# Image 0's query and key convolutions by a two-level scheme

## The chip, the cores and the metric

One core of a Trainium2 chip runs the whole program in one launch. The metric is device time in microseconds: lower is better. Times of before are the median of three runs; a profiled execution shows what each engine did.

## The reference, cut to what matters

Eight images of 512 channels and 32 x 32 = 1024 places go through two attention blocks, all in fp32. The first block has 32 groups in its norm and 8 heads, the second 8 groups and one head.

```python
# block 0
h = group_norm(x, gn_weight, gn_bias)                      # 32 groups
qkv = einsum('oc,bct->bot', w_qkv, h) + b_qkv              # 3 x 512 by 512, a matrix product per image
q, k, v = per head (64 channels each)
weight = softmax(einsum('bct,bcs->bts', q * scale, k * scale))
a = einsum('bts,bcs->bct', weight, v)
x = x + einsum('oc,bct->bot', w_proj, a) + b_proj
# block 1, one head of 512 channels
xn = group_norm(x, gamma, beta)                            # 8 groups
q, k, v = conv1x1(xn, q_w), conv1x1(xn, k_w), conv1x1(xn, v_w)
x = x + conv1x1(softmax(q @ k * scale) @ v, p_w)
```

What the change touches is the product of the 512 x 512 query and key weights with the normed image 0 (512 x 1024) in block 0.

## The kernel before

**Matrix products in halves.** Every large product uses Winograd's form of Strassen's scheme: both operands are cut into 2 x 2 quarters, sums of quarters are made (four sums for each operand), and seven products of quarters take the place of eight; the results are added up on the way out of PSUM. The sums are named by the product they serve: for weights 1 is a11, 2 is a12, 3 is s4, 4 is a22, 5 is s1, 6 is s2, 7 is s3 (`left_sums`); for images 1 is b11, 2 is b21, 3 is b22, 4 is t4, 5 is t1, 6 is t2, 7 is t3 (`right_sums`). `ORDER = (1, 5, 2, 6, 7, 3, 4)` is the order in which they lie in a weight tile.

*Once in halves:* `conv` (through `by_channel` and `wino`) does a convolution in seven steps, each of four matmul calls of 512 columns, that is eight matmul records in the trace. `by_token` does the same for the values, with tokens on the rows. `wino` takes a list of steps (`middle`), runs some entries of the `background` list after each step (`back` of them), and leaves its steps 4 and 3 on a list `tail`, which the next stage runs after its own first step (`finish()`).

*Twice in halves:* `conv2` splits each of the seven products again in seven: 49 products of a 128 x 128 weight with 256 columns. It takes them in four groups (`pair`): products 1 and 5 together, then 2 and 6, then 7 with 3 and 4 begun inside it, each group with seven inner steps (`inner_steps`). `hooks[s]` are functions that run after group s (s = 0, 1, 2 and 3; in the code the group of 3 and 4 is s = 3 and that of 7 is s = 2). Its image factors come from `inner_factors` (L434): four subtractions of 128 x 256 for each of the seven outer factors. Its weight factors are second sums, which lie in DRAM (`wdram2`) and are loaded in two parts by `load_weight`. Some results are added together by GpSimd (`more`, L571), the others by VectorE (L564, L566) from PSUM, and ScalarE adds the bias halves (L578).

**Before, image 0 is the exception.** The prologue holds it: the image's values, queries and keys are computed once in halves, since their second sums are made only there. `prepare(n)` loads a weight into one of three slots of `wpool` and gives four steps on VectorE for the first sums (L291, L292). `keep2` makes the second sums (four `tensor_tensor` of 128 x 896, L318, into tiles of their own) and stores seven parts of 448 KB in DRAM for the later images: v's on VectorE, q's, k's, m's and p's on GpSimd. All later images use `conv2`.

**The prologue in order.** Raw k and q weights, image 0 and the v, q and k weights are loaded; k and q are transposed (`natural`), the norm's statistics are taken, and the product m of q and k weights is made (`product`). Then the value convolution, the query convolution, the key convolution; meanwhile image 1's statistics (`x1`, L91) and the sums of m. Then the value weights are transposed (`tr_wv`), the bias products are made from natk, raw p and raw p0 (`bias_products`), then the product z, and the attention of image 0 starts.

**What sets the order.** A scheduler places the instructions of each engine ahead of the run; the order on each engine is fixed then. Whatever is wrapped in `keep_in_program_order` stays behind what was traced before it on its engine. All matmuls are wrapped, so PE runs in the written order. Loads and stores go through SP's queue. Working tiles of 4 KB a partition come from a pool `big` of `NBIG = 34`.

```python
tail.extend([lambda: step(4), lambda: step(3), *after])          # wino: left to the next stage
w = weights2[s // 2][:, (0, 2, 0, 1)[s] :]                       # conv2: weights from the loaded tiles
```

## Time and profile before

| | |
|---|---|
| median of 3 runs | 2768.14 us (2767.19 to 2768.42) |
| profiled execution, its own time | 2768.3 us |
| its span | 2765.8 us |
| PE busy | 2753.6 us |
| VectorE (DVE) busy | 2045.6 us |
| GpSimd (POOL) busy | 1291.4 us |
| ScalarE (ACT) busy | 998.4 us |
| value convolution of image 0 | 25.25 to 49.50 us |
| query and key convolutions of image 0 | 49.50 to 97.56 us |
| first attention of image 0 starts | 117.85 us |

In the profile PE is the matmul unit, PEld its weight loads, SP the engine that issues most DMAs. A row of the order of time has start, length, engine, line, operation, `out<-in`, the shape, and in brackets the idle time before it with what ended it. A row of waits has the total, the number and the longest. A row of stretches has the stretch, its length, then busy time (and instructions) of PE, PEld, DVE, ACT and POOL, the granted clock, DMA's busy share and GB/s. All matmuls have line L60 and all transposes L63, so they are told apart by the tiles they write: `psa_q`, `psb_q` and `psc_q` are the PSUM banks of the query convolution, and so on.

### The profile page before, as it was taken

The numbers are of one execution on the slowest core, as the hardware profiler recorded it, in microseconds if no ns is written. First come the engines' busy times: TensorE is split into PE (matmuls) and PEld (weight loads), VectorE is DVE, ScalarE is ACT, GpSimd is POOL, SyncE is SP. The second block draws the span as 40 slices with busy tenths as digits, with TensorE's granted clock in tenths as the row PEclk, the third lists the DMA queues.
The fourth block names the chain that finished last, engine by engine and source line by source line (L and its number), as shares of the span: only waits on it lengthen the run. The fifth ranks groups of instructions, "written<-read, shape, count | busy, mean of one in ns | idle before, by whom it ended". The sixth has DMA issues, their size and how long they took to land.

```text
span 2765.8 us, 36809 instructions
## 1 busy us (share of the span) xinstructions
PE 2753.6 (100%) x13436; PEld 1762.1 (64%) x13436; DVE 2045.6 (74%) x3214; ACT 998.4 (36%) x1307; POOL 1291.4 (47%) x1384
## 2 busy tenths in 40 slices
PE   9999999999999999999999999999999999999999
PEld 5437736776376853868538694486844968348585
DVE  6587777777777777777777867777678776787776
ACT  1253454214632146312453125531255313633130
POOL 2313605745067440774307752176621766146763
PEclk9999999999999999999999999999999999999999
DMA  7827412344113441144401443114521145112302
GB/s 265 253 91 252 181 32 70 138 159 166 40 63 138 170 162 32 63 161 167 150 24 63 177 182 119 32 55 184 196 98 49 58 153 216 59 54 97 142 24 74
DMA packets 126070, 332.60 MB, mean 120 GB/s; under 512 B 19831, under 2 KB 64695, under 8 KB 114362
## 3 DMA queue, kind: packets, MB, share of 16 engines
q1 hardware_dynamic: 125294, 329.75, 33.6%
q8 instruction: 108, 1.77, 0.3%
q14 instruction: 80, 0.66, 0.1%
q10 hardware_dynamic: 588, 0.42, 0.1%
HBM read 258.14 MB, written 71.99 MB: 119 GB/s over the span
## 4 chain that ended last, share of the span: by engine, by line
PE 99%; DVE 1%; DMA 0%; issue 0%; SPq 0%; DVEq 0%
PE sc L60 16%; PE av L60 16%; PE psb_av L60 6%; PE psb L60 5%; PE psa_av L60 4%; PE psc_av L60 4%; PE psc L60 4%; PE psa L60 3%; PE psb_v L60 3%; PE psb_k L60 3%; PE psb_p L60 3%; PE psb_q L60 3%; PE psb_g L60 3%; PE psb_z L60 3%; PE psc_z L60 2%; PE psa_k L60 2%
## 5 line engine op out<-in xcount | busy, mean ns | idle before, releaser
L700 DVE TENSOR_TENSOR sum<-sum,e 128x1024 f32<-128x1024 f32 x384 | 473.9, 1234 | 35.5 <-ACT e L696 0.9
L696 ACT ACTIVATE e<-sc 128x1024 f32<-128x1024 f32 x512 | 476.1, 1053 | 63.1 <-PE sc L60 62.6
L60 PE MATMUL sc<-q,k 64*128 64x512 f32 x2048 | 456.8, 596 | 0.0
L60 PE MATMUL av<-e,v 128*64 128x512 f32 x2048 | 453.4, 595 | 0.0
L60 PEld LDWEIGHTS sc<-q,k 64*128 64x128 f32 x2048 | 190.1, 185 | 245.9 <-ACT e L696 120.9
L60 PEld LDWEIGHTS av<-e,v 128*64 128x64 f32 x2048 | 141.4, 137 | 299.0 <-issue 288.2
L434 POOL TENSOR_TENSOR inner_h<-x 128x256 f32<-128x256 f32 x16 | 14.8, 924 | 415.9 <-DVE x L1028 415.9
L698 DVE TENSOR_TENSOR sum<-e,e 128x1024 f32<-128x1024 f32 x64 | 79.9, 1249 | 103.6 <-ACT e L696 103.6
L719 ACT COPY a<-av 128x512 f32<-128x512 f32 x64 | 37.5, 586 | 320.1 <-PE av L60 280.6
L126 POOL TENSOR_TENSOR rstd<-ve,mhalf 128x4 f32<-128x4 f32 x16 | 18.8, 1177 | 274.0 <-DVE ve L124 274.0
L60 PE MATMUL psb<-inner,inner_h 128*128 128x256 f32 x448 | 115.6, 380 | 0.0
L60 PE MATMUL psa_av<-e,z 128*128 128x512 f32 x256 | 112.5, 592 | 0.0
L482 ACT COPY psb_v<-psa_v 128x512 f32<-128x512 f32 (+1 forms) x28 | 14.5, 517 | 232.5 <-DVE x L845 176.6
L60 PEld LDWEIGHTS psb<-inner,inner_h 128*128 128x128 f32 x448 | 84.5, 190 | 13.6 <-POOL inner L449 2.1
L60 PE MATMUL psb_z<-w_z,inner_h 128*128 128x128 f32 x672 | 87.5, 276 | 0.0
L60 PE MATMUL psb_g<-inner_h,w_m 128*128 128x256 f32 x336 | 84.9, 381 | 0.0
L776 ACT ACTIVATE e<-e 128x1024 f32<-128x1024 f32 x64 | 65.1, 1052 | 46.7 <-DVE e L766 25.6
L60 PEld LDWEIGHTS psb_z<-w_z,inner_h 128*128 128x128 f32 x672 | 81.4, 192 | 0.5
L60 PEld LDWEIGHTS psa_av<-e,z 128*128 128x128 f32 x256 | 47.4, 190 | 53.6 <-issue 51.7
L771 POOL TENSOR_TENSOR e<-e,e 128x512 f32<-128x512 f32 x64 | 79.3, 1271 | 2.0 <-DVE e L766 1.8
L571 POOL TENSOR_TENSOR v<-v,v 128x256 f32<-128x256 f32 x28 | 20.1, 726 | 125.3 <-DVE u_v L566 121.3
L820 POOL TENSOR_TENSOR t<-e,t 128x1024 f32<-128x1024 f32 x32 | 78.4, 2482 | 0.0
(443 smaller groups left out, 6138.0 us busy)
## 6 DMA issues: line engine op xcount, KB each, us to landing
r<-all_rows SPq DMA_DIRECT2D x78, 256.0 KB
x<-in_x SPq DMA_DIRECT2D x36, 512.0 KB
h<-in_x SPq DMA_DIRECT2D x32, 512.0 KB
spill<-x SPq DMA_DIRECT2D x32, 512.0 KB
x<-spill SPq DMA_DIRECT2D x32, 512.0 KB
out<-x SPq DMA_DIRECT2D x63, 256.0 KB
kept<-a SPq DMA_DIRECT2D x28, 512.0 KB
again<-kept SPq DMA_DIRECT2D x28, 512.0 KB
```

The source lines that it names most:

```text
L60: tc.keep_in_program_order(nc.tensor.matmul(*args, **kw))
L126: nc.gpsimd.tensor_tensor(rstd, ve, mhalf, ALU.pow)
L434: pin(engine.tensor_tensor(dst, x, y, ALU.subtract))
L482: nc.scalar.copy(ps["b"], ps["a"])
L571: nc.gpsimd.tensor_tensor(d, x, y, ALU.add)
L696: nc.scalar.activation(e, sc, AF.Exp, scale=(C // 8) ** -0.5)
L698: nc.vector.tensor_add(total, es[0], e)
L700: nc.vector.tensor_add(total, total, e)
L719: nc.scalar.copy(dst, av)
L771: nc.gpsimd.tensor_tensor(blocks(dst, r, cc)[0], blocks(x, r, cc)[0], blocks(y, r, cc)[0], ALU.add)
L776: nc.scalar.activation(e[c, cc, r], e[c, cc, r], AF.Exp, scale=scale)
L820: on = lambda *a: lambda: tc.keep_in_program_order(nc.gpsimd.tensor_tensor(*a))
```

## The change

- q and k of image 0 are computed by `conv2`, with the weights' second sums taken from SBUF, where they have just been made (`own`), and not from DRAM. No weight is loaded for it.
- The image's inner factors (7 x 4 subtractions of 128 x 256) are made by GpSimd while PE does the value convolution.
- `keep2_steps` becomes `second_sums`: with `inside=True` it puts the sum s3 in the place of a21 and takes three tiles of `big` for the others, and it also returns a function that picks a factor. q's second sums move from GpSimd to VectorE, into the value convolution; k's stay on GpSimd, in the hooks of the query convolution; v's move from VectorE to GpSimd, in the hooks of the key convolution.
- k's first sums move from the query convolution into the value convolution (`back` is 6, not 4).
- Image 1's loads move into the query convolution's second hook, its statistics into the third, in halves; the raw v and p loads and m's loads move into the key convolution's second hook, m's first sums into its fourth.
- `NBIG` is 35, not 34, and the identity takes the place of a line of sums (`rpool`). `all_background` is defined earlier.

```diff
-NBIG = 34
+NBIG = 35
...
-        def keep2_steps(n, t, engine=nc.gpsimd, pin=lambda ins: ins):
-
-            if engine is nc.gpsimd:
-                u = wpool.tile([P, 4, 7, P], F32, tag="w", name=f"prepare2_{n}")
-                u = [u[:, i, :, :] for i in range(4)]
-            else:
-                u = [big_tile(f"prepare2_{n}_{i}", (P, 7, P)) for i in range(4)]
+        def second_sums(n, t, engine, pin=lambda ins: ins, inside=True):
+
             quarter = lambda k, i: t[:, :, k, ts(i, P)]
             a11, a21, a12, a22 = quarter(0, 0), quarter(0, 1), quarter(1, 0), quarter(1, 1)
-            s1, s2, s3, s4 = u
+            if inside:
+                s3 = a21
+                s1, s2, s4 = (big_tile(f"prepare2_{n}_{i}", (P, 7, P)) for i in range(3))
+            else:
+                u = wpool.tile([P, 4, 7, P], F32, tag="w", name=f"prepare2_{n}")
+                s1, s2, s3, s4 = (u[:, i, :, :] for i in range(4))
+            f2 = (a11, a12, s4, a22, s1, s2, s3)
+
             def store():
-                for j, f in enumerate((a11, a12, s4, a22, s1, s2, s3)):
+                for j, f in enumerate(f2):
                     pin(nc.sync.dma_start(wdram2[n][:, :, j, :], f))
 
-            return [
+            return lambda p, j: f2[j - 1][:, ORDER.index(p), :], [
...
-        def conv2(n, f, bias, name, hooks=(), after=(), by_tokens=False, alone=False):
+        def conv2(n, f, bias, name, hooks=(), after=(), by_tokens=False, alone=False, own=None):
...
-                w = weights2[s // 2][:, (0, 2, 0, 1)[s] :]
+                def weight_of(i, j):
+                    if own:
+                        return own(products[i], j)
+                    return weights2[s // 2][:, (0, 2, 0, 1)[s] + i, j - 1, :]
...
-            ident.append(big_tile("ident", (P, P)))
+            ident.append(rpool.tile([P, 2, 2, P], F32, tag="line", bufs=1, name="ident")[:, 0, 0, :])
...
-            raw_v = raw("v", 6)
-            raw_p = raw("p", 7)
             for f in first["v"][1]:
                 f()
-            background.extend(steps)
-            background.extend(first["q"][1])
-            v = by_token(weight_factors(first["v"][0]), hf, "v0_0", middle=(2, 5, 6, 7), back=4)
+            in_order = tc.keep_in_program_order
+            inner, ih = inner_factors(hf, "h0_0", in_order)
+            wq2, q_sums = second_sums("q", first["q"][0], nc.vector)
+            background.extend([*steps, *first["q"][1], *ih[:2], *q_sums[:4], *first["k"][1], *ih[2:], q_sums[4]])
+            v = by_token(weight_factors(first["v"][0]), hf, "v0_0", middle=(2, 5, 6, 7), back=6)
+            all_background()
+            norm1, x1, made = GroupNorm(0, "0_1"), [], {}
+
+            def load_x1():
+                x1.extend(load_x(1, c, "x1") for c in range(KC))
+
+            def half_stats(c, i):
+                norm1.half_stats(c, i, x1[c][:, ts(i, HT)])
+                if i:
+                    norm1.end_stats(c)
+
+            def stats():
+                background.extend(lambda c=c, i=i: half_stats(c, i) for c in range(KC) for i in range(2))
+
+            def load_raw():
+                made["v"], made["p"] = raw("v", 6), raw("p", 7)
+
+            def prepare_m():
+                made["m"] = prepare("m")
+
+            def sum_m():
+                for f in made["m"][1]:
+                    f()
+
+            wk2, k_sums = second_sums("k", first["k"][0], nc.gpsimd)
+            q = conv2("q", inner, pcols("bq0"), "q0_0", [k_sums[:2], [load_x1], [*k_sums[2:], stats]], own=wq2)
+            _, v_sums = second_sums("v", first["v"][0], nc.gpsimd)
+            k = conv2(
+                "k", inner, pcols("bk0"), "k0_0",
+                [v_sums[:2], [all_background, load_raw, prepare_m], v_sums[2:], [sum_m]], own=wk2,
+            )
             finish()
-            run_background(len(background))
-            keep2("v", first["v"][0], nc.vector)
-            background.extend(first["k"][1])
-            x1 = [load_x(1, c, "x1") for c in range(KC)] if B > 1 else []
-            norm1 = GroupNorm(0, "0_1")
-            background.extend(lambda c=c: norm1.stats(c, x1[c]) for c in range(len(x1)))
-            q = conv(weight_factors(first["q"][0]), hf, pcols("bq0"), "q0_0")
-            keep2("q", first["q"][0])
-            keep2("k", first["k"][0])
-            t, steps = prepare("m")
-            k = conv(weight_factors(first["k"][0]), hf, pcols("bk0"), "k0_0", hooks=[[], [], [], [], steps])
-            finish()
+            raw_v, raw_p, t = made["v"], made["p"], made["m"][0]
```

More of the change, by code (lines that the diff above doesn't have):

```diff
@@ L219, in run_background, with all_background @@
                 background.pop(0)()
+        def all_background():
+            run_background(len(background))
         tail = []
@@ L325, in keep2_steps, with keep2 @@
             ]
-        def keep2(n, t, engine=nc.gpsimd):
-            for f in keep2_steps(n, t, engine):
+        def keep2(n, t):
+            for f in second_sums(n, t, nc.gpsimd, inside=False)[1]:
                 f()
@@ L585, in written @@
                     return [(t, 2 * i + r) for t, (i, _) in zip(to, y)]
-                w = weights2[s // 2][:, (0, 2, 0, 1)[s] :]
+                def weight_of(i, j):
+                    if own:
+                        return own(products[i], j)
+                    return weights2[s // 2][:, (0, 2, 0, 1)[s] + i, j - 1, :]
                 def mm(ps, j, start):
                     for i, p in enumerate(products):
-                        wt = w[:, i, j - 1, :]
+                        wt = weight_of(i, j)
                         if not by_tokens:
@@ L613, in conv2 @@
             second = []
-            weights2 = [weight_part((n, 0))]
+            load = [] if own else [load_weight]
+            weights2 = [] if own else [weight_part((n, 0))]
             pair(0, (1, 5), [(1, 0), (1, 1)], None, [])[1]()
             pair(
-                1, (2, 6), [(0, 0), (0, 1)], [(1, 0), (1, 0)], [load_weight, lambda: biased_half(0, 0)], defer=second,
+                1, (2, 6), [(0, 0), (0, 1)], [(1, 0), (1, 0)], [*load, lambda: biased_half(0, 0)], defer=second,
             )[1]()
-            weights2.append(weight_part((n, 1)))
+            if not own:
+                weights2.append(weight_part((n, 1)))
             ahead, end = pair(
-                3, (3, 4), [(0, 1), (1, 0)], [(0, 1), (1, 0)], [load_weight, *after],
+                3, (3, 4), [(0, 1), (1, 0)], [(0, 1), (1, 0)], [*load, *after],
                 order=(-3, 6, 5, -4, 7, 2) if alone else (-3, 6, -4, 2, 5, 7),
@@ L991, in prologue @@
             load = lambda: load_weight(tc.keep_in_program_order)
-            second = keep2_steps("z", t, pin=tc.keep_in_program_order)
+            _, second = second_sums("z", t, nc.gpsimd, tc.keep_in_program_order, False)
             later = {
@@ L1011, in load_again @@
             return t
-        def all_background():
-            run_background(len(background))
         def begun(load, norm, b, what):
```

## The prediction

> **What bounds the kernel.** I read the engine shares first, then PE's waits over the whole span, then PE's order of time around image 0's convolutions, then the table of stretches. Shares of the page, PE's waits, three rows of PE's order of time (start, length), and stretches (length, then busy time of each engine):

> ```profile
> PE 2753.6 (100%) x13436; PEld 1762.1 (64%) x13436; DVE 2045.6 (74%) x3214; ACT 998.4 (36%) x1307; POOL 1291.4 (47%) x1384
> ...
> PE tr_wk L63 <- DMA rawk<-in_w: 3.8, 1, 3.8
> PE tr_wv L63 <- DVE k L410: 0.5, 1, 0.5
> PE ps_wm L60 <- DVE natq L900: 0.5, 1, 0.5
> PE psb_v L60 <- DVE u_v L566: 0.5, 1, 0.5
> ...
> 49.50 3.60 PE L60 MATMUL psa_q<-h,prepare_q 128*128 128x512 f32 x8
> 52.93 3.60 PE L60 MATMUL psb_q<-t_h,prepare_q 128*128 128x512 f32 x8
> ...
> 97.56 0.49 PE L63 MATMUL tr_wv<-ident,rawv 128*128 128x128 f32 x3
> ...
> 49.50:97.56 48.06, 48.06 (x113) 21.23 (x112) 32.55 (x44) 5.09 (x8) 18.01 (x8) 1.00 0.81 258
> ...
> 277.74:298.89 21.15, 21.15 (x99) 18.62 (x98) 16.49 (x36) 6.52 (x11) 20.03 (x28) 1.00 0.42 152
> ```

> PE is busy almost throughout, and its longest wait after the first load is 0.5 us; all other engines run beside it. So only removed PE work saves time, and at most some 2 us of waits could go besides. Image 0's query and key convolutions fill 49.50 to 97.56: 14 steps, one every 3.43 us. The last line is image 1's query convolution, which already has the form of the change (halves twice): 21.15 us from its first product to that of the next one, with no PE wait in it.

> [...]so I price PE by the distance from one convolution's start to the next, not by busy time. [...]the trace shows 0.69 and 1.08 to 1.09 us, so I use the trace's. [...]DVE, then GpSimd, in order of time:

> ```profile
> 55.04 0.69 DVE L240 TENSOR_TENSOR u_q<-psb_q,t_q 128x512 f32<-128x512 f32 x1
> ...
> 58.13 4.46 DVE L292 TENSOR_TENSOR prepare_k<-prepare_k 128x512 f32<-128x512 f32 x2
> ...
> 232.91 2.35 DVE L1028 TENSOR_TENSOR t_h<-h,t_h 128x512 f32<-128x512 f32 x2
> 235.19 1.75 DVE L734 TENSOR_TENSOR a<-a,r 128x1024 f32<-128x1024 f32 x1
> ...
> 54.66 9.87 POOL L318 TENSOR_TENSOR prepare_q<-prepare_q 128x896 f32<-128x896 f32 x4 [29.40 <-DMA sums_v<-prepare_v]
> ...
> 233.66 1.06 POOL L434 TENSOR_TENSOR inner_h<-h,inner_h 128x256 f32<-128x256 f32 x1
> 234.68 1.17 POOL L434 TENSOR_TENSOR inner_h<-h,h 128x256 f32<-128x256 f32 x1
> 235.82 1.70 POOL L434 TENSOR_TENSOR inner_h<-h,inner_h 128x256 f32<-128x256 f32 x1
> ```

> Two SBUF sums of DVE that take 1.29 us alone take 4.46 beside GpSimd; a GpSimd inner subtraction takes 0.72 alone (as at 237.49), 1.17 when it alternates with a 512-column DVE sum and 1.70 with a 1024-column one. The sum at 55.04 reads PSUM and keeps its 0.69[...].

> **The change, part by part.**

> *PE.* Removed: 2 x 7 steps x 3.43 = 48.06 us. Added: 2 x 49 products of 256 columns; one such convolution takes 21.15 us, so 42.30. Net -5.76 us, if nothing is late. All the rest can only take from this. The first products of the new query convolution run before the last two steps of the value convolution, near 42.6; those two take 6.9 us, so the key convolution ends near 42.6 + 6.9 + 42.3 = 91.8, and the transposes of the value weights start there instead of at 97.56.

> *GpSimd, in 25 to 55.* Added: 7 x 4 inner subtractions. GpSimd is idle there (its first work after 25.3 is at 54.66). Alone they take 28 x 0.72 = 20.2 us. The first two groups are needed at 50.5 (the value steps hide them), the next two at about 55, the last three from 60: even with all 14 DVE sums of the stretch between them they end near 55, so PE does not wait for them.

> *DVE, in 25 to 50.* Added: q's four second sums, 4 x 1.0; k's four first sums move here, 4 x 0.6. Removed: v's four second sums at 50.3 to 54.5 go to GpSimd. DVE has room (13.4 us busy of the 25 from 25 to 50)[...]: from 25.7, 10 sums of 512 columns at 1.17 and four of 896 at about 1.6 (between 1.17 and 1.70) end at 43.8 instead of 35.7. The eviction of step 6 comes ready at 37.68 and PE reuses that bank at 39.14, a slack of 0.77 us after its 0.69. If evictions, which are not pinned to the order, are put between the sums, they come at most about one locked sum late: 0 to 1 us. If all sums stand ahead of them: 43.8 - 37.7 - 0.77 = 5.3 us. No gain is possible here, as PE has no wait to lose. I take 0.4, range 0 to 5.3.

> *DVE in the query convolution.* Such evictions take 12.4 us of 21 (image 1's key convolution); x1's statistics add 8 x 0.62 + 4 x 0.2 = 5.8. Image 1's value convolution carries such statistics too and lost 0.17 + 0.45 us to late evictions. I take 0.3, range 0 to 0.8; ACT and the bias adds hide behind PE as in image 1.

> *GpSimd, 55 to 92.* k's and v's second sums, four of 2.08 us each, and 2 x 8 additions of 0.73: 16.6 + 11.7 = 28 us of the 37 up to 92, so there is room; k's third and fourth sums, behind q's additions, should be ready near 70 and are needed near 74 and 76. Cost nothing; a lag of over 4 us would show.

> *SP and its transfers.* No byte is added. In before the raw value and projection weights are issued from 22.66 and 26.38, and nothing moves from 42 to 51. These (2 MB, 5.8 us at the 360 GB/s that weight loads reach) now go behind x1's loads, k's stores and x1's statistics, whose tiles they take over: x1 issued near 58, landed near 66, counted by 78; raw value weights issued near 81 and landed by 86, the projection's near 89, m's by 92. Needed: 91.8 and 94.4. Covered by 3 to 6 us. The third load, raw p0, is issued from 90.44 in before; it stands behind the layer-0 projection's tile, which needs one of three weight slots: q's goes to m, v's comes free only when its sums are stored, k's when the key convolution ends. If it is issued ahead of that, it lands by 94; if behind it, at 96 to 98, and the bias products, all pinned in PE's order and the next PE work after the transposes, wait from 94.4. I take 0.5, range 0 to 6. Stores of q's sums move earlier (near 44 to 50, where nothing moved before).

> *After 118.* The first attention starts about 5 us earlier; image 1's loads do not all move. ACT's scaling of h waits 0.68 us for them at 141.23, and ACT's next copy is at 146.13: 3.7 us of slack hide most of it. 0, range -0.5 to 1. The larger tile pool, the moved identity and the shared closure: 0, nothing on PE waits for a big tile in before; the gap of 0.5 at the transposes stays, as the same banks are emptied.

> Sum: -5.76 + 0.4 + 0.3 + 0.5 = -4.6 us, against the profiled execution's 2768.3 (its span 2765.8 and 2.5 around it). That execution stands 0.16 over the median of 2768.14, so 2763.5.

> **Rivals.** [...]DVE's pinned sums stand ahead of the value convolution's evictions, +5.3 instead of +0.4, which gives 2768.4. For it: 14 sums against 28 subtractions in one stretch; against: evictions are free to move up, and in before they were put between k's first sums (55.04, 57.53).

> *Transfers come last and it is slower.* Place: bias products, on raw p0, behind a weight slot. GpSimd is some 6 us late, ends v's sums at 96, their four stores (448 KB at the 290 GB/s of such stores, 1.6 us each) free the slot at 102, two loads of 2.9 us land raw p0 at 108 to 110, PE waits about 15: -5.8 + 15 gives 2777. It decides from a landing at 94.4 + 5.8 = 100.2 (no gain) and 105.7 (slower by 0.2%). For it: in before raw weights were in place long ahead; against: 28 us of DMA idle before 145 and stores of unchanged quarters that can go early.

> *It does not cut PE:* if the pairs of 256-column products ran slower with weights out of strided tiles, nothing would change, 2768. Image 1's 21.15 us speaks against it.

> **How the numbers follow.** A measurement of this kernel can tell about 0.2%, 5.5 us, so even the full -5.76 barely counts as faster. As summed, with up to 1.2 us more or less: 0.55, of which 0.33 lies beyond -5.5 (all waits near zero). Still better through small waits gone, to -6.6: 0.03. Part or all lost to lock or a late load, 2765 to 2771: 0.27. Slower by transfers: 0.12. No cut: 0.03. So faster 0.36, same 0.52, slower 0.12. The range goes from 2761.5 (-6.6) to 2769.5, which leaves out the slower rival and the end of the third case.

> **What would show it.** Right: q and k products of 128x256 in 42.3 us, transposes of the value weights near 92, inner subtractions of 0.72 to 1.7 us ending near 55, no PE wait over 1 us. Wrong: a PE wait at psb_v for u_v (lock), at tr_wv or ps_bias for a raw weight (transfers), at psa_k to psc_k for k's sums (GpSimd).

## The result, and the profile after

The changed kernel takes 2782.99 us (median of 6 runs, 2780.71 to 2784.70) against 2768.28 us: ratio 1.0053, 95% interval 1.0040 to 1.0066. It is slower by 0.5%, and the prediction of 2763.5 us was wrong in sign and size. The profiled execution's own time is 2784.7 us, its span 2782.9.

First the engine shares of the page, then PE's waits over the whole span (total, number, longest):

```profile
PE 2756.7 (99%) x13520; PEld 1785.5 (64%) x13520; DVE 2061.2 (74%) x3254; ACT 1007.7 (36%) x1323; POOL 1333.5 (48%) x1428
```

```profile
PE tr_wv L63 <- DVE k L569: 5.2, 1, 5.2
PE tr_wk L63 <- DMA rawk<-in_w: 4.7, 2, 3.9
PE psb_v L60 <- DVE u_v L243: 4.6, 1, 4.6
PE psb_k L60 <- ACT psb_k L487: 2.2, 1, 2.2
PE psc_v L60 <- DVE x L855: 1.7, 2, 1.0
```

There is less product work, yet PE is *busier* than before (2756.7 against 2753.6 us). Three waits are new: 4.6 us in the value convolution, 2.2 near the start of the key convolution, 5.2 at the transposes. They make 12 us. The rest is in how long the matmuls behind them take. PE's order of time:

```profile
45.50 5.96 PE L60 MATMUL psb_v<-prepare_v,h 128*128 128x256 f32 x16 [4.59 <-DVE u_v L243]
...
55.62 3.62 PE L60 MATMUL psc_v<-prepare_v,h 128*128 128x256 f32 x16
...
83.52 1.37 PE L60 MATMUL psb_k<-inner_h,prepare_k 128*128 128x256 f32 x4 [2.19 <-ACT psb_k L487]
...
111.44 3.44 PE L63 MATMUL tr_wv<-ident,rawv 128*128 128x128 f32 x15 [5.23 <-DVE k L569]
```

The 16 matmuls behind the first wait take 5.96 us; 16 of the same shape take 3.62 ten us later. The stretches say why; the granted clock is the third number from the end (then DMA share and GB/s):

```profile
58.20:105.94 47.74, 45.14 (x197) 37.89 (x196) 30.51 (x71) 12.39 (x21) 23.56 (x21) 0.96 0.56 178
...
39.84:43.25 3.41, 1.07 (x5) 0.59 (x4) 3.38 (x4) 0.00 (x0) 3.33 (x3) 1.00 0.90 275
43.25:46.67 3.42, 1.17 (x3) 0.99 (x4) 3.41 (x5) 0.00 (x0) 3.42 (x4) 0.50 0.96 287
46.67:50.08 3.41, 3.41 (x10) 2.70 (x9) 3.39 (x4) 0.00 (x0) 3.33 (x4) 0.50 0.94 283
50.08:53.49 3.41, 3.41 (x18) 3.00 (x17) 2.46 (x4) 0.00 (x0) 3.33 (x6) 1.00 0.92 283
...
80.80:84.21 3.41, 1.22 (x6) 0.80 (x5) 2.84 (x8) 1.80 (x3) 3.30 (x3) 1.00 0.82 224
84.21:87.63 3.42, 3.42 (x9) 2.70 (x9) 0.00 (x0) 1.17 (x2) 2.07 (x1) 0.50 1.05 347
...
104.69:108.11 3.42, 1.52 (x7) 0.84 (x6) 3.42 (x5) 0.72 (x1) 3.42 (x3) 1.00 0.65 194
108.11:111.52 3.41, 0.08 (x1) 0.11 (x2) 3.19 (x5) 0.72 (x1) 2.65 (x3) 0.50 1.01 291
111.52:114.93 3.41, 3.41 (x17) 3.41 (x17) 0.66 (x2) 0.44 (x1) 3.33 (x3) 0.50 1.00 330
```

The stretches of 3.41 us are cut where the granted clock changes. Each of the three waits is followed by half clock, for 6.83, 3.41 and 6.83 us. Part of that time lies in the waits themselves; after PE has started again, at 45.50, 83.52 and 111.44, 4.58, 3.42 and 3.49 us of it are left. From start to start two matmuls of 128x256 take 0.86 us there (`psa_k`, 84.68 to 85.54) and 0.44 at full clock (88.73 to 89.17), so half of that is lost: some 2.3, 1.7 and 1.7 us (an estimate from these times).

The first line stands for the query and key convolutions: 47.74 us where the prediction had 42.30. It begins 0.87 us ahead of `psb_q` at 59.07, as four records of the query convolution have already run among the value convolution's last steps.

Laying the two traces beside each other from the start of each stage gives the whole account of the profiled executions (the extra beyond a wait is the stage's length less the expected length less its waits):

| stage | before | after | difference, and what it holds |
|---|---|---|---|
| start to value convolution | 25.25 | 26.86 | +1.61; it lies between 24.78 and 26.86 in the traces of all kernels here. PE waits a second time for the raw k weights in this one (0.84 us, up to 7.57), and full clock is granted from 12.53 us on, in before from 6.90 |
| value convolution | 24.25 | 31.34 | +7.09 = 4.59 wait + 2.50 beyond it (some 2.3 at half clock) |
| query and key convolutions | 48.06 | 47.74 | -0.32 = -5.76 products + 2.60 waits (2.19, 0.24, 0.17) + 2.84 beyond them (some 1.7 at half clock, the rest around the waits at full clock) |
| transposes, to the bias products | 2.70 | 9.08 | +6.38 = 4.71 more wait + 1.67 at half clock |
| to the first attention | 17.59 | 17.58 | 0 |
| all later images | | | +2.20 |

In sum +16.9, of which 11.9 are waits, 7.0 lie beyond them (5.7 of it at half clock, by the estimate above), 2.2 later and 1.6 at the start, against -5.76. The medians differ by 14.7.

### The profile page after: what moved, and what is told of

Its sections match the earlier page's. It is cut to its first block, busy times and chain, and to the rows that moved or that the text cites. A ratio compares the mean times of both kernels' runs of the same rounds, so it can differ in the third digit from the quotient of the medians.

```text
span 2782.9 us, 37118 instructions
## 1 busy us (share of the span) xinstructions
PE 2756.7 (99%) x13520; PEld 1785.5 (64%) x13520; DVE 2061.2 (74%) x3254; ACT 1007.7 (36%) x1323; POOL 1333.5 (48%) x1428
## 4 chain that ended last, share of the span: by engine, by line
PE 95%; DVE 3%; issue 1%; DMA 1%; POOL 0%; SPq 0%; ACT 0%; DVEq 0%; POOLq 0%
PE sc L60 16%; PE av L60 16%; PE psb L60 5%; PE psb_av L60 5%; PE psa_av L60 4%; PE psc L60 4%; PE psa L60 3%; PE psc_av L60 3%; PE psb_p L60 3%; PE psb_g L60 3%; PE psb_z L60 3%; PE psb_k L60 3%; PE psb_v L60 3%; PE psb_q L60 3%; PE psc_z L60 2%; PE psa_g L60 2%
## 5 line engine op out<-in xcount | busy, mean ns | idle before, releaser
L60 PE MATMUL sc<-q,k 64*128 64x512 f32 x2048 | 456.8, 596 | 0.0
L60 PE MATMUL av<-e,v 128*64 128x512 f32 x2048 | 453.4, 595 | 0.0
L60 PEld LDWEIGHTS sc<-q,k 64*128 64x128 f32 x2048 | 191.4, 186 | 244.6 <-ACT e L706 113.2
L60 PEld LDWEIGHTS av<-e,v 128*64 128x64 f32 x2048 | 141.4, 137 | 299.0 <-issue 277.6
L60 PE MATMUL psb<-inner,inner_h 128*128 128x256 f32 x448 | 115.6, 380 | 0.0
L60 PE MATMUL psa_av<-e,z 128*128 128x512 f32 x256 | 112.5, 592 | 0.0
L60 PEld LDWEIGHTS psb<-inner,inner_h 128*128 128x128 f32 x448 | 84.5, 190 | 13.6 <-POOL inner L454 2.1
L60 PE MATMUL psb_z<-w_z,inner_h 128*128 128x128 f32 x672 | 87.5, 276 | 0.0
L60 PE MATMUL psb_g<-inner_h,w_m 128*128 128x256 f32 x336 | 84.9, 381 | 0.0
L576 POOL TENSOR_TENSOR k<-k,k 128x256 f32<-128x256 f32 x32 | 25.5, 807 | 119.2 <-DVE u_k L571 116.1
L60 PEld LDWEIGHTS psa_av<-e,z 128*128 128x128 f32 x256 | 47.4, 190 | 53.6 <-issue 51.7
L60 PEld LDWEIGHTS psb_z<-w_z,inner_h 128*128 128x128 f32 x672 | 81.4, 192 | 0.5
```

Source lines behind the costliest of these rows:

```text
L60: tc.keep_in_program_order(nc.tensor.matmul(*args, **kw))
L576: nc.gpsimd.tensor_tensor(d, x, y, ALU.add)
```

## The experiments

**Theory.** Three links are late, each through its place in an engine's order: (1) DVE's four sums of q, which take 1.50 to 1.60 us each beside GpSimd's inner subtractions and took 1.08 to 1.09 without them in before (v's, from 50.31), stand ahead of the evictions of step 6; (2) k's third and fourth sums stand ahead of q's last additions on GpSimd, and ScalarE's copy for `psb_k` stands behind bias halves that wait for those; (3) at the key convolution's end v's last sums (GpSimd) and m's first sums (DVE) stand among k's last additions and evictions. Each wait is followed by a stretch at half clock. **Rivals:** the scheme itself costs PE time with weights out of strided tiles, or the transfers moved are late. *Lock* and *locked* in the recorded texts name the slowing in (1), as measured, and no cause of it. The rows of DVE and of GpSimd for (1), in the changed kernel:

```profile
38.76 1.50 DVE L323 TENSOR_TENSOR prepare_q<-prepare_q 128x896 f32<-128x896 f32 x1
40.29 1.50 DVE L323 TENSOR_TENSOR prepare_q<-prepare_q,prepare_q 128x896 f32<-128x896 f32 x1
41.71 1.60 DVE L323 TENSOR_TENSOR prepare_q<-prepare_q 128x896 f32<-128x896 f32 x1
43.24 1.60 DVE L323 TENSOR_TENSOR prepare_q<-prepare_q,prepare_q 128x896 f32<-128x896 f32 x1
44.77 1.28 DVE L243 TENSOR_TENSOR u_v<-psb_v,t_v 128x512 f32<-128x512 f32 x2
```

```profile
40.80 1.57 POOL L439 TENSOR_TENSOR inner_h<-t_h 128x256 f32<-128x256 f32 x1
42.45 1.45 POOL L439 TENSOR_TENSOR inner_h<-t_h,inner_h 128x256 f32<-128x256 f32 x1
```

One sum and one subtraction alternate, four pairs in 6.01 us; `u_v` starts at 44.77; its bank is ready near 39.3 (12.4 us after the value convolution's start, as in the next experiment).

**1. No inner subtractions**, the inner factors being quarters of h:

```diff
-            inner, ih = inner_factors(hf, "h0_0", in_order)
+            inner = {}
+            for p in ORDER:
+                b11, b12, b21, b22 = (hf[p][kk][:, ts(i, 2 * P)] for kk in range(2) for i in range(2))
+                inner[p] = {1: b11, 2: b21, 3: b22, 4: b21, 5: b11, 6: b22, 7: b12}
+            ih = [lambda: None] * 7
```

> The changed kernel with GpSimd's 28 inner subtractions left out: the inner factors are replaced by the plain quarters, so image 0's queries and keys are other numbers; every product and every DVE instruction stays. Theory (lock): the sums of DVE ahead of the first eviction of step 6 take 0.6 and 1.0 us again, DVE is there in time, PE's wait of 4.6 us at psb_v for u_v goes, and with it the 2.5 us in which PE runs at a lower granted clock: 7 us less than the changed kernel, near 2776. Rival (order alone): DVE's order by itself makes the eviction late, the wait stays at 3 us or more and the time stays within 3 us of 2783.

2774.68 us, 1.0023 (1.0016 to 1.0030), 8.3 less than the changed kernel. DVE, the last sum of q and the first eviction:

```profile
35.19 1.08 DVE L323 TENSOR_TENSOR prepare_q<-prepare_q,prepare_q 128x896 f32<-128x896 f32 x1
37.76 0.69 DVE L243 TENSOR_TENSOR u_v<-psb_v,t_v 128x512 f32<-128x512 f32 x1 [1.49 <-PE psb_v L60]
```

Without GpSimd's subtractions the sums take 1.08, DVE waits for PE and not PE for DVE, and the wait at `psb_v` is gone, all as the theory had it. That it is these subtractions that slow the sums is shown; the waits of 2.2 and 5.2 stay and are not theirs.

**2. q's second sums on GpSimd**, between its inner subtractions:

```diff
-            wq2, q_sums = second_sums("q", first["q"][0], nc.vector)
-            background.extend([*steps, *first["q"][1], *ih[:2], *q_sums[:4], *first["k"][1], *ih[2:], q_sums[4]])
+            wq2, q_sums = second_sums("q", first["q"][0], nc.gpsimd)
+            background.extend([*steps, *first["q"][1], *ih[:2], *q_sums[:4], *ih[2:], q_sums[4], *first["k"][1]])
```

> The changed kernel with q's four second sums on GpSimd, between the inner subtractions of products 1, 5 and those of 2, 6, and k's first sums last. Theory: without the four long sums ahead of it the eviction of step 6 comes in time, PE's wait at psb_v goes with its slow clock, -7 us, near 2776; the waits at psb_k (2.2) and tr_wv (5.2) stay. Rival (GpSimd becomes the bound): with 28 x 0.7 and 4 x 2.1 us GpSimd ends near 60 and PE waits for inner factors at psb_q to psc_q, 2 us or more, which gives 2778 to 2783.

2781.45 us, 1.0048 (1.0031 to 1.0065): no gain beyond a microsecond or two. The wait at `psb_v` is gone, but one of 6.2 us at `psb_q` takes its place. DVE:

```profile
70.30 0.69 DVE L91 BATCH_NORM_STATS2 bnst<-x 128x6 f32<-128x512 f32 x1 [6.52 <-DMA x<-in_x]
70.91 0.41 DVE L571 TENSOR_TENSOR q<-psa_q,q 128x256 f32<-128x256 f32 x1
```

The statistics of image 1 stand ahead of q's evictions here, and image 1 is not there yet: its load, behind the stores of q's and k's sums, is issued from 65.41 on, in the changed kernel from 61.21. So DVE's order held up the evictions once more, behind another instruction. The rival had the time right, but not the cause: no wait for an inner factor is in the trace.

**3. m's first sums after the key convolution** and not in its fourth hook:

```diff
-                [v_sums[:2], [all_background, load_raw, prepare_m], v_sums[2:], [sum_m]], own=wk2,
+                [v_sums[:2], [all_background, load_raw, prepare_m], v_sums[2:]], own=wk2,
...
             finish()
+            sum_m()
```

> The changed kernel with m's four first sums on DVE moved from the key convolution's last hook to behind its last evictions. Theory: the wait of 5.2 us at tr_wv is k's evictions behind m's sums, which alternate with GpSimd's sums of v; it falls to 0.5 as before the change, and the slow clock behind it (1.7 us) goes too: -6.4 us, near 2776.6. Rival (the raw value weights or v's sums are late themselves): the wait at tr_wv stays above 3 us with another releaser, and the time within 2 us of 2783.

2782.18 us, 1.0051 (1.0034 to 1.0068): 0.8 less where the theory had 6.4. PE:

```profile
106.64 1.83 PE L63 MATMUL tr_wv<-ident,rawv 128*128 128x128 f32 x15 [2.79 <-DVE k L569]
...
112.83 0.59 PE L60 MATMUL ps_bias<-rawp,par 128*1 128x512 f32 x1 [1.57 <-DMA rawp<-in_w]
```

m's sums are 2.4 of the 5.2 us; the other 2.8 come from k's additions behind v's sums (0.5 of it was there in before). The 15 transposes take 1.83 us, so no half clock followed this wait. The second line is the raw p0 load of the prediction, issued in part behind v's stores: hidden behind the longer wait in the changed kernel, it appears once that shrinks. In the trace 4.1 us are saved up to the bias products, and 2.6 of it are given back between there and the first attention.

**4. All four of k's second sums in the query convolution's first hook**:

```diff
-[k_sums[:2], [load_x1], [*k_sums[2:], stats]]
+[k_sums[:4], [load_x1], [k_sums[4], stats]]
```

> The changed kernel with all four second sums of k in the query convolution's first hook, while GpSimd is idle, and not two of them behind its third group. Theory: the wait of 2.2 us at psb_k is ScalarE's bias of q, which waits for GpSimd's last additions of q, which stand behind k's third and fourth sums; ScalarE's copy to psb_k comes in time, the wait goes and the slow clock behind it (some 2 us) too: -4.5 us, near 2778.5. Rival (DVE's statistics of x1 hold up the same evictions): a wait at psb_k or psc_q of 1.5 us or more stays, and the time within 2 us of 2783.

2778.73 us, 1.0036 (1.0024 to 1.0049), 4.3 less than the changed kernel, as expected: the wait at `psb_k` of link 2 is gone, 2.19 us and some 1.7 at half clock behind it. The other two waits are unchanged.

**5. Only the third link**, with all of v's sums in the first hook and m's behind the end:

```diff
-                made["v"], made["p"] = raw("v", 6), raw("p", 7)
+                made["v"], made["p"], made["p0"] = raw("v", 6), raw("p", 7), raw("p0", 3)
...
-                [v_sums[:2], [all_background, load_raw, prepare_m], v_sums[2:], [sum_m]], own=wk2,
+                [v_sums, [all_background, load_raw, prepare_m], []], own=wk2,
...
             finish()
+            sum_m()
```

> The changed kernel with only its third late link moved: all of v's second sums in the key convolution's first hook, m's first sums behind the key convolution's end, raw p0 loaded behind raw v and raw p. Theory (the additions of k that stand behind v's last two sums, and m's first sums among the evictions, make the 5.2 us together): the wait at tr_wv falls to 0.5 to 1.1 us with no half clock behind it; the waits of 4.6 at psb_v and 2.2 at psb_k stay; 5.5 to 7 us less than the changed kernel's 2782.8, that is 2776 to 2777.5. Rival (raw v behind v's stores is late then): a wait for rawv at tr_wv of 1 to 4 us takes its place, 2778 to 2782.

2777.82 us, 1.0033 (1.0020 to 1.0046), 5.2 less, a little short of the 5.5 expected; the wait at `tr_wv` is 1.02, nothing is late for `ps_bias`. The other two waits of the changed kernel remain, at 4.6 and 2.2. So each link is shown by itself: the first in experiment 1, the second in 4, the third here.

**6. The place of q's sums**: all four behind step 6's evictions.

```diff
-[*steps, *first["q"][1], *ih[:2], *q_sums[:4], *first["k"][1], *ih[2:], q_sums[4]]
+[*steps, *first["q"][1], *ih[:6], *q_sums[:4], ih[6], q_sums[4], *first["k"][1]]
```

> The changed kernel with q's second sums still on VectorE, but put behind the sixth inner subtraction in the list, so that they stand after the first evictions of the value convolution's step 6 and before those of its later quarter. Theory (what makes the 4.6 us wait is the place of the four locked sums ahead of the first eviction of u_v): the wait at psb_v for u_v goes, and a shorter one, up to 3.3 us, comes at psb_v for w_v, which now stands behind the sums; the waits of 2.2 at psb_k and 5.2 at tr_wv stay; 1 to 4 us less than the changed kernel's 2782.8. Rival (the number of sums under the lock decides, whatever their place): a wait of 4 to 5 us stays somewhere in the value convolution and the time is 2782 to 2784.

2780.95 us, 1.0043 (1.0029 to 1.0057), 2.0 less than the changed kernel. PE:

```profile
47.31 5.41 PE L60 MATMUL psb_v<-prepare_v,t_h 128*128 128x256 f32 x16 [3.14 <-DVE w_v L243]
```

The wait moved one quarter on and shrank from 4.6 to 3.1, as the theory said; the number of sums alone would have kept it.

**7 and 8. A wait made on purpose in the kernel before**: seven and eleven more 128x1024 subtractions on DVE, pinned ahead of step 6's evictions:

```diff
+            def hold():
+                for _ in range(7):   # 11
+                    tc.keep_in_program_order(nc.vector.tensor_sub(idle, h0[0], h0[1]))
+            background.insert(12, hold)
```

In both, the evictions of this convolution in `wino` are also kept in program order, and `back` is 5, not 4.

> The kernel before, with seven additional subtractions of 128x1024 on VectorE (into a tile that nothing reads) in image 0's value convolution, pinned ahead of the evictions of its step 6: a short PE wait at psb_v, made on purpose. Theory (a short wait costs itself alone): a wait of 1 to 2 us, granted clock stays at 1.00 behind it, total above before by the wait, 2769 to 2770. Rival (any wait costs a stretch at half clock): some 1.7 us more, 2771 to 2772.

> As the one with seven, but eleven subtractions: a wait of 5.5 to 6.5 us at psb_v. Theory (a wait of several us is followed by about 3.4 us at half clock, in which the matmuls take twice as long): total above before by the wait and 1.7 to 2.5 us more, 2775.5 to 2777, with the clock near 0.5 to 0.7 in the 3 us behind the wait and matmuls psb_v that take over 4 us for 8 in place of 3.6. Rival (the loss is the wait alone): 2774 to 2774.7, clock 1.00.

2772.57 us, 1.0016 (1.0009 to 1.0022), and 2778.93 us, 1.0038 (1.0024 to 1.0052). PE of the first, then of the second:

```profile
41.82 3.72 PE L60 MATMUL psb_v<-prepare_v,h 128*128 128x256 f32 x16 [1.97 <-DVE u_v L240]
```

```profile
46.20 6.61 PE L60 MATMUL psb_v<-prepare_v,h 128*128 128x256 f32 x16 [7.02 <-DVE u_v L240]
```

A wait of 1.97 delays all later PE work by 2.24, at full clock throughout; one of 7.02 delays it by 10.17, and the clock is 0.50 from 41.84 to 52.08 us. The first wait cost 0.27 us beyond its length, the second 3.15, in a kernel without the change; if 0.27 of that is again no matter of the clock, the half clock cost 2.9 (an estimate from these two), and the 5.88 us of half clock that are left after 46.20 say the same (half of them is 2.94). Wait, clock loss and total all came out larger than expected for the second kernel. The first kernel's total rose by 4.3, more than its 2.24, and so into the range of the rival; the granted clock of 1.00 speaks against that rival all the same. Its profile shows PE's work ending 2.7 us later and the span 5.4 longer, the rest behind the last eviction; that excess is not explained.

**9. All three links moved**: q's sums on GpSimd, image 1 loaded before the value convolution, k's and v's sums each in one first hook, m's sums late, raw p0 early. The edits of experiments 2 and 5, image 1's statistics pinned to their order (`pinned=True`), and:

```diff
+            x1 = [load_x(1, c, "x1") for c in range(KC)]
             v = by_token(weight_factors(first["v"][0]), hf, "v0_0", middle=(2, 5, 6, 7), back=6)
...
-[k_sums[:2], [load_x1], [*k_sums[2:], stats]]
+[k_sums, [], [stats]]
```

> The changed kernel with all three late links moved: q's second sums to GpSimd between its inner subtractions (x1 loaded ahead of the value convolution, so that its statistics hold up nothing), all of k's second sums in the query convolution's first hook, all of v's in the key convolution's first hook, m's first sums after the key convolution's end, raw p0 loaded behind raw v and raw p. Theory (three late links, each a wait and a stretch at half clock behind it): no PE wait over 1 us between 25 and 130, granted clock 1.00 there, about 5.8 us less than before, 2762 to 2764, ratio 0.998 to 0.999. Rival 1 (the scheme itself costs PE time with weights out of strided tiles): waits gone, but query and key convolutions stay over 44 us and the total stays at or over 2768. Rival 2 (another thing is late once these are not, raw weights or image 1's loads): a new PE wait of 1 to 6 us at tr_wv, ps_bias or psb_q, 2766 to 2773.

2770.79 us, 1.0010 (1.0003 to 1.0016), 12 less than the changed kernel, but some 7 over what was expected. PE:

```profile
70.89 1.91 PE L60 MATMUL psb_q<-inner_h,prepare_q 128*128 128x256 f32 x4 [2.09 <-DVE u_q L571]
```

GpSimd, with q's sums among the inner subtractions, ends k's sums only at 69.4, and q's additions behind them are late: 2.09 of wait, and half clock from 71.09 to 74.51 (some 1.7 us lost). Rival 2 had named this bank and this time, but other causes. Rival 1 falls: from 50.94 on, 82 matmul records in a row take 17.7 us, 0.216 each; with 98 to a convolution that is 42.3 for both.

**10. q's sums on DVE again, spread**: one behind step 6's evictions, three behind step 7's (four empty entries, `nothing`, shift them there).

```diff
-[*steps, *first["q"][1], *ih[:2], *q_sums[:4], *ih[2:], q_sums[4], *first["k"][1]]
+[*steps, *first["q"][1], *ih[:6], q_sums[0], ih[6], *nothing, *q_sums[1:], *first["k"][1]]
```

> As the kernel with all three links moved, but q's second sums back on VectorE and spread: the first behind the evictions of the value convolution's step 6, the other three behind those of step 7, so that GpSimd's inner subtractions and k's second sums end some 6 us earlier and q's additions are not late. Theory: the wait of 2.1 us at psb_q for u_q and the half-clock stretch of about 2.3 us behind it go, no wait over 1.1 us is left between 25 and 130, the query and key convolutions take 42.3 to 43.5 us; the first attention starts 4 to 5 us earlier than in that kernel, 2765 to 2767 in all, ratio 0.998 to 1.000 against before. Rival 1 (q's late sums come too late for its second inner step): a wait of 1 to 4 us at psb_q or psc_q near 51, 2767 to 2772. Rival 2 (PE's products are slower in this form): no wait, yet over 45 us for the two convolutions.

2768.73 us, 1.0002 (0.9994 to 1.0010): the level of before, over the 2765 to 2767 expected. No wait brings half clock here. Its largest waits in the stage:

```profile
PE psc_q L60 <- DVE v L403: 1.4, 1, 1.4
PE tr_wv L63 <- DVE k L569: 1.0, 1, 1.0
PE psc_q L60 <- DVE c_q L571: 0.8, 1, 0.8
```

**11. The last short waits**: k's last three first sums behind the value evictions, image 1's statistics in the key convolution, the transposes in other banks, and the evictions of the values (L403) pinned to their order.

```diff
-            q = conv2("q", inner, pcols("bq0"), "q0_0", [k_sums, [], [stats]], own=wq2)
+            background.extend([*[lambda: None] * 6, *first["k"][1]])
+            q = conv2("q", inner, pcols("bq0"), "q0_0", [k_sums, [], []], own=wq2)
...
-                [v_sums, [all_background, load_raw, prepare_m], []], own=wk2,
+                [[*v_sums, stats], [all_background, load_raw, prepare_m], []], own=wk2,
...
-            wv = natural(raw_v, "v", "bc")
+            wv = natural(raw_v, "v", "ac")
```

> As the kernel with q's second sums spread, with its remaining waits taken away: k's last three first sums behind the value convolution's last evictions and ahead of the first of the query convolution's, image 1's statistics in the key convolution's second group instead of among q's last evictions, and the transposes of the value weights into the banks of psa and psc, so that they needn't wait for psb_k. Theory (what is left of the gain is in these short waits and nothing else): psc_q 1.4 and 0.8, psb_q 0.3 and tr_wv 1.0 go, no wait over 0.5 us between 25 and 118, the first attention starts 3 to 3.5 us earlier than in that kernel, near 113.5, and the total is 2764.5 to 2766.5, ratio 0.9985 to 0.9995. Rival (statistics or first sums make other evictions late): a wait of 0.5 to 3 us at psb_q, psc_q or psc_k, 2767 to 2770.

2764.97 us against 2768.18, ratio 0.9988 (0.9981 to 0.9995): 0.12% below before and below the changed kernel, as expected. Its PE waits, without those under 0.6 (the last is a little over the 0.5 expected):

```profile
PE tr_wk L63 <- DMA rawk<-in_w: 4.1, 2, 3.7
PE psc_v L60 <- DVE x L855: 1.8, 2, 1.1
PE psc_k L60 <- DVE c_k L571: 0.7, 1, 0.7
```

From the value convolution's start to the first attention it takes 87.74 us where before takes 92.60, that is -4.86: -4.12 up to the transposes, out of the -5.76, and -0.74 at the transposes, where the other banks also take away before's wait of 0.5. In the profiled execution the later images give 3.0 of it back.

**The later images.** In the changed kernel PE's work is 2.20 us later at the end than at the first attention, in two steps. DVE, then PE, at the first:

```profile
923.81 0.69 DVE L91 BATCH_NORM_STATS2 bnst<-ahead 128x6 f32<-128x512 f32 x1 [0.83 <-DMA ahead<-in_x]
```

```profile
929.64 1.16 PE L60 MATMUL psc_v<-w_v,inner_h 128*128 128x128 f32 x8 [0.60 <-DVE x L855]
```

A part of the next image's load lands late, its statistics stand in DVE's order ahead of the bank's eviction, and PE waits. The experiments on the changed kernel lose 1.4 to 3.4 us in the later images, 0.7 to 2.8 of it in waits for the same instruction; before loses nothing there, with the same issues in the same order around it. Of the two kernels with a wait made on purpose, whose code behind is that of before, the first loses nothing and the second 1.1. So the change's code is not needed for it; why the transfer is late there was not tried.

## Why the prediction was wrong

- **PE, -5.76: right.** Experiment 9 shows the rate, experiment 11 has 4.12 of it in the time. "It does not cut PE" falls.
- ***DVE in 25 to 50*, taken 0.4, range 0 to 5.3: the failed step that began it.** It cost 7.09. The upper bound was good for the wait (5.3; measured 4.59). The value taken rested on "evictions are free to move up". They are, but the order is fixed ahead of the run, and here it put all four sums ahead of `u_v`. In the kernel before such evictions lay between sums; that was no evidence for another set of sums. The rival with all of DVE's sums ahead of the evictions had this right and stopped at the wait: the 2.50 us behind it were missing, in it and in every other term.
- ***GpSimd, 55 to 92*, "cost nothing": failed, the other way round.** It cost a wait of 2.19 and some 1.7 at half clock. It asked whether k's third and fourth sums would be ready behind q's additions. In the trace they stand *ahead* of q's last ones. GpSimd (first fence) and ScalarE (second) of the changed kernel:

```profile
77.88 2.08 POOL L323 TENSOR_TENSOR prepare_k<-prepare_k,prepare_k 128x896 f32<-128x896 f32 x1
79.92 0.72 POOL L576 TENSOR_TENSOR q<-q 128x256 f32<-128x256 f32 x1
```

```profile
80.68 0.72 ACT L583 ACTIVATE q<-q,par 128x512 f32<-128x512 f32 x1 [7.45 <-POOL q L576]
82.17 0.72 ACT L583 ACTIVATE q<-q,par 128x512 f32<-128x512 f32 x1 [0.77 <-POOL q L576]
82.80 0.58 ACT L487 COPY psb_k<-psa_k 128x512 f32<-128x512 f32 x1
```

  A sum that nobody yet needs holds an addition, that a bias half, and that the copy PE waits for. Room on GpSimd was counted in busy time (28 of 37 us); who stands behind whom was not.
- **The gap at the transposes, "stays, as the same banks are emptied": failed.** m's first sums, which the change moves into the key convolution's fourth hook, were not costed at all. DVE there:

```profile
107.04 3.08 DVE L295 TENSOR_TENSOR prepare_m<-prepare_m 128x512 f32<-128x512 f32 x3
110.04 0.47 DVE L569 SCALAR_TENSOR_TENSOR k<-psc_k,par,u_k 128x256 f32<-128x256 f32 x1
```

  With v's last sums ahead of k's additions they made 5.23 us out of 0.5, plus 1.67 at half clock.
- ***DVE in the query convolution*, 0.3: right**, 0.24 and 0.17.
- ***SP and its transfers*, 0.5: no cost** in the changed kernel, where the raw weights were in time and raw p0 lay behind another wait; experiment 3 brought it out as a wait of 1.57, within the range. The rival that ended slower named this place; that it came out slower was right by another mechanism, so its 2777 came nearer by luck.
- ***After 118*, 0, range to 1: too small**, 2.20; late image loads are seen in it.

The term that no step had is the clock. In the changed kernel it was granted at 0.50 behind each of the three waits, for 6.83, 3.41 and 6.83 us, and it changes only at multiples of 3.41 us, whatever the waits. PE was not idle for the whole of the 3.41 us before a fall: that stretch still holds 1.07, 1.22 or 1.52 us of work. The last section has the count over all runs.

## What to carry to other kernels

When PE is bound by nothing else, a step moved onto a busy helper engine is priced by its neighbours in that engine's order: for each moved instruction ask which eviction, addition or copy now stands behind it and when PE needs that, not only whether the engine has room. Put sums that are needed late behind the evictions that are needed now, in the order written out, and don't trust a scheduler to lift them past pinned work. Waits of 2.09 to 7.02 us brought half clock on top in these runs (one of 2.79 did not), which cost 1.7 to 2.9 us by the estimates above, so one of 4.6 cost 7.1; three small orderings ate a saving of 5.8 us three times over.

## What the runs showed of the hardware

- Of the windows at full clock up to PE's last matmul, 18 were followed by half clock: 17 in which PE was busy for 39% or less, one at 45%. Every window busy for 50% or more kept full clock; so did the only other one below that, at 43%. If the share is what decides, the bound lies between 39 and 50% (an estimate from these counts), and these traces can't place it more closely, as the ends of matmuls are modelled.
- Half clock ended each time behind a window in which PE was busy throughout. The 11 windows behind which it went on had PE busy for 72% or less.

So length alone did not decide: waits of 2.09 us (experiment 9), 2.19, 4.59 and 5.23 (the changed kernel), 3.14 (experiment 6) and 7.02 (experiment 8) were followed by half clock; 1.9 (experiment 6, in the later images), 1.97 (experiment 7) and 2.79 (experiment 3) were not. The last was cut in two by the grid, and PE was busy for 50 and 68% of the two windows:

```profile
102.15:105.56 3.41, 1.70 (x8) 1.01 (x6) 1.73 (x5) 0.72 (x1) 3.33 (x4) 1.00 0.57 180
105.56:108.97 3.41, 2.33 (x23) 2.01 (x26) 3.06 (x7) 1.41 (x3) 0.41 (x1) 1.00 1.00 260
```

By an estimate from the 39 and 50%, a window was lost once some 1.7 to 2.1 us of its 3.413 were idle. A single wait under 1.7 us would then lose none, one over twice 2.1 us would lose at least one, and in between it is a matter of where the grid falls; full clock is first granted at 6.90 us in before and at 12.53 in the changed kernel, which is no whole number of windows apart.

**DVE and GpSimd beside each other.** The prediction's 0.69 and 1.08 to 1.09 us are DVE's times for sums of 512 and 896 columns; with GpSimd idle, before shows 0.68 (at 29.33) and 1.08 to 1.09 (from 50.31). In the changed kernel the period of a pair is neither engine's own time nor their sum: a DVE sum of 128x896 (1.08 alone) and a GpSimd subtraction of 128x256 (0.72 alone) alternate every 1.50 us on the mean (38.76 to 44.77 for four pairs), where whole instructions in turn would take 1.80. The two evictions of `u_v` from PSUM, at 44.77, were not slowed: they took 1.28 us together, and the subtraction beside them, at 45.39, kept its 0.72. Why sums and subtractions slow each other was not shown.
